# First-stage tiles laid into attention's late tiles, one step of values formed behind attention's first scores, and a changed order of the first loads

## The chip, the cores and the metric

The kernel runs on one core of one Trainium2 chip. The metric is device time in microseconds (us) of one execution, as the median of several. The core has a matrix engine (TensorE, PE in the profile, with PEld for its weight loads), a vector engine (VectorE, DVE), an activation engine (ScalarE, ACT), a general engine (GpSimd, POOL) and SyncE (SP), whose only work here is to issue transfers. SyncE, ScalarE and GpSimd each issue DMAs in the order of their own instruction streams: an instruction that waits holds up everything queued behind it on its engine.

## The reference, cut to what matters

The model has two layers on a feature map x of shape 4 x 384 x 32 x 32. What the change touches is the attention of the first layer, 8 heads of 48 channels, with relative-position tables:

```
x    = x + conv0(_ln_c(x))
xt   = x.reshape(b, c, n).transpose(0, 2, 1)                # _ln_c has been applied
qkv  = (xt @ w_qkv).reshape(b, n, 3, HEADS, hd)             # n = 1024, hd = 48
attn = q*scale @ k^T + gather(q*scale @ table_k^T) + gather(k*scale @ table_q^T)^T
attn = softmax(attn)
out  = attn @ v + (attn summed by relative position) @ table_v
out  = out @ w_proj + b_proj
```

Behind it come a small feed-forward part, a depthwise convolution and a mixture of four experts of which each token takes two. The change leaves their arithmetic alone. The experts' input buffer in DRAM (xs_d) is filled with zeros during attention, and that filling is touched.

## The kernel before, in words

Three phases run one after the other: `qkv_phase`, `attention_phase`, `rest_phase`. All arithmetic is in 32-bit floats.

**`qkv_phase`** goes over the 4096 tokens in 8 steps of 512 (t = 0 to 7 in the code; the texts here say step 1 to step 8). A step loads its tokens `xt` (L155), takes their mean and variance (`token_stats`: PE transposes L87, VectorE L89 and L90, ScalarE's square root L96, VectorE's reciprocal L97), spreads the reciprocal deviation over the partitions (`to_partitions`: VectorE L115 builds a diagonal `s_dg`, PE L117 multiplies it into `all_ps`, ScalarE L168 copies it to `scale`), forms q and k (36 matmuls, L174), scales them on VectorE (L178) into `qk_sb` and stores them to `qk_d` by GpSimd (L179). Then it takes the statistics of the *next* step, and last forms its own v: for each of four blocks of 128 tokens six matmuls (L185) and a ScalarE copy (L188) into `va`, which GpSimd stores to `v_d` (L193, 1 MB a step). The order inside this phase is not written out: the framework's scheduler orders each engine's instructions by readiness in its own model of time, earlier lines first. In the trace it sets two matmuls of v before the last three transposes of the next step's statistics, which wait for a PSUM buffer. The phase's tiles (`wq`, two `va`, three `xt`, `scale`, `s_dg`, four `qk_sb`) live in pools of their own, which end with the phase; so do its PSUM buffers.

**`attention_phase`** goes over 8 heads. Here the order is written out by hand: nearly every instruction goes through `pin`, `mm`, `dma` (SyncE, L226) or `bulk` (ScalarE, L229), which keep it behind the instruction traced before it on its engine. For the first head, `load_tables` and `load_keys` fetch q, k and the tables; `prepare` multiplies q and k with the tables (L221, `tabq_ps` and `tabk_ps`), 32 of each; VectorE transposes one product into the tile `b2` (L316), ScalarE copies the other (L320) into `st`, and SyncE stores it to the DRAM buffer `sd`. Then the head's 32 image rows are worked one by one. For a row:

- `fetch` loads the row's 240 KB from `sd` into `s1` (three buffers) on SyncE, and GpSimd adds it to `b2` (L351, three instructions a row at most) into `bias` (three buffers);
- `queries` loads `qs` for two rows on SyncE (two buffers, so the one for rows 6 and 7 waits for the scores of row 3);
- `scores`: 16 matmuls (L221, `sc_ps`, two PSUM buffers, so the scores of a row wait for `biased` of the row two before);
- `biased`: VectorE adds the bias and takes the minimum (L379) into `arow` (three tiles; rows 0 to 5 and 38 to 43 of each are padding that stays zero);
- `exponentials`: ScalarE (L389); `far_sums`: VectorE (L400); `transposes`: PE L408 and ScalarE L409 into `aT`; `windows`: PE L418 and ScalarE L427 into `a1t`; every fourth row `values`: 64 matmuls with `vb` (L221, `av_ps`).

`load_values` fetches `vb` (four transfers of 256 KB, one for each image of the batch) and `load_value_table` fetches `tvw` (15 transfers, one a row from row 1 on), both on SyncE. `clear` writes zeros to `xs_d`, 64 transfers of 384 KB in all. The tiles `vb`, `aT`, `a1t` and `tvw` of the pool `late` are first written only after the first scores.

The start of a head, before the change:

```
            for s in blk[:3]:
                fetch(s)
            for _ in load_values(h):
                pass
...
            scores(blk[0])
            scores(blk[1])
...
            biased(blk[0])
            exponentials(blk[0])
```

and in the loop over the rows y `queries(blk, y + 4)` (at even y) stands ahead of `fetch(blk[y + 3])`.

Of the kernel before, what the change touches and what calls it, by code (L numbers as in the profile page):

```python
# [11 lines left out]
F32 = mybir.dt.float32  # L12
# [6 lines left out]
P = 128  # L19
# [12 lines left out]
YB = 4  # L32
# [77 lines left out]
def to_partitions(nc, pools, ident, one, values):  # L110

    small, psum, tag = pools
    nj = values.shape[1]
    dg = small.tile([P, nj, P], F32, tag="s_dg", name="s_dg", bufs=1)
    nc.vector.tensor_tensor(dg, bcast(ident.unsqueeze(1), 1, nj), bcast(values, 2, P), ALU.mult)  # L115
    ps = psum.tile([P, TOK], F32, tag=tag, name="all_ps")
    nc.tensor.matmul(ps, one, dg.rearrange("p j n -> p (j n)"), start=True, stop=True)  # L117
    return ps
# [14 lines left out]
def qkv_phase(tc, cst, x, w_qkv, qk_d, v_d):  # L133
# [5 lines left out]
    one, ident = cst["one"], cst["ident"]  # L139
    with ExitStack() as es:  # L140
        wp = es.enter_context(tc.tile_pool(name="q_w", bufs=1))
        work = es.enter_context(tc.tile_pool(name="q_work", bufs=2))
        ev = es.enter_context(tc.tile_pool(name="q_ev", bufs=4))
        psum = es.enter_context(tc.tile_pool(name="q_ps", bufs=3, space=PSUM))
        psmm = es.enter_context(tc.tile_pool(name="q_mm", bufs=4, space=PSUM))
        vas = [wp.tile([P, HEADS, TOK // P, VW], F32, name=f"va{i}") for i in range(2)]
        for va in vas:
            nc.vector.memset(va, 0.0)
        wq = wp.tile([P, KC, 3 * C], F32, name="wq")
        xts = {}  # L150

        def load(t):
            b, n0 = divmod(t * TOK, N)
            xts[t] = work.tile([P, KC, TOK], F32, tag="xt", name="xt", bufs=3)
            nc.sync.dma_start(xts[t], x[b, :, n0 : n0 + TOK].rearrange("(k p) n -> p k n", p=P))  # L155
# [6 lines left out]
        for t in range(NT // TOK):  # L162
# [3 lines left out]
            ps = to_partitions(nc, (work, psum, "st"), ident, one, rstd)  # L166
            scale = work.tile([P, TOK], F32, tag="scale", name="scale")
# [3 lines left out]
            for m in range(2 * KC):  # L171
                ps = psmm.tile([P, TOK], F32, tag="mm", name="qk_ps")
                for k in range(KC):
                    nc.tensor.matmul(  # L174
                        ps, wq[:, k, m * P : (m + 1) * P], xt[:, k, :], start=(k == 0), stop=(k == KC - 1)
                    )
                sb = ev.tile([P, TOK], F32, tag="qk", name="qk_sb")
                nc.vector.tensor_tensor(sb, ps, scale, ALU.mult)  # L178
                nc.gpsimd.dma_start(qk_d[m * P : (m + 1) * P, t * TOK : (t + 1) * TOK], sb)  # L179
            if t + 1 < NT // TOK:  # L180
                stats = result(token_stats(nc, (work, psum, "st"), ident, xts[t + 1], cst["eps6"]))
            for j in range(TOK // P):
                ps = psmm.tile([P, TOK], F32, tag="mm", name="v_ps")
                for k in range(KC):
                    nc.tensor.matmul(  # L185
                        ps[:, :C], xt[:, k, j * P : (j + 1) * P], wq[:, k, 2 * C :], start=(k == 0), stop=(k == KC - 1)
                    )
                nc.scalar.activation(  # L188
                    vas[t % 2][:, :, j, :HD], ps[:, :C].rearrange("p (h d) -> p h d", d=HD),
                    AF.Copy, scale=rstd[:, j, :],  # L190
                )
            w = NBLK // 2 * VW
            nc.gpsimd.dma_start(  # L193
                v_d.rearrange("h p n -> p h n")[:, :, t * w : (t + 1) * w],
                vas[t % 2].rearrange("p h c d -> p h (c d)"),
            )


def attention_phase(tc, cst, held, tabs, tv, qk_d, v_d, ao_d, xs_d, heads):
# [31 lines left out]
    with ExitStack() as es:  # L231
        dram = es.enter_context(tc.tile_pool(name="a_dram", bufs=2, space=DRAM))
        late = es.enter_context(tc.tile_pool(name="a_late", bufs=1))
# [9 lines left out]
        vb = late.tile([P, B, NBLK, VW], F32, name="vb")  # L243
        aT = late.tile([P, NBLK, YB, P], F32, name="aT")
        a1t = late.tile([P, 4, IMG, YT, B], F32, name="a1t")
        tvw = late.tile([P, 4, IMG, HD], F32, name="tvw")
# [11 lines left out]
        zero = fixed.tile([P, 1, C], F32, name="zero")  # L258
        nc.gpsimd.memset(zero, 0.0)
# [262 lines left out]
        def clear():  # L522

            rows = 2 * P
            for n0 in range(0, NEXP * CAP, rows):
                dma(
                    xs_d[n0 : n0 + rows].rearrange("(n p) c -> p n c", p=P), bcast(zero, 1, rows // P),
                )
                yield
# [14 lines left out]
        for n, h in enumerate(heads):  # L544
# [10 lines left out]
            for _ in load_values(h):  # L555
                pass
            if n:
                for g in (1, 2):
                    add_table(batch[1], g, value_table(g, ps_t))
            scores(blk[0])  # L560
            scores(blk[1])
            if n:
                po = value_table(3, ps_o)
            biased(blk[0])
# [8 lines left out]
            for y in range(IMG):  # L573
                s, r = blk[y], y % YT
                if y % 2 == 0 and y + 4 < IMG:
                    queries(blk, y + 4)
                if y + 3 < IMG:
                    fetch(blk[y + 3])
                if batch and y == 3:
# [930 lines left out]
def metaformer_kernel(ctx: ExitStack, tc: tile.TileContext, ins, out):  # L1510
# [19 lines left out]
    with tc.tile_pool(name="held", bufs=1) as pool:  # L1530
# [4 lines left out]
        qkv_phase(tc, cst, ins["x"], ins["w_qkv"], qk_d, v_d)  # L1535
        attention_phase(tc, cst, held, ins["tabs"], ins["tv"], qk_d, v_d, ao_d, xs_d, list(range(HEADS)))
# [72 lines left out]
```

## Time and profile before

| what | us |
|---|---|
| median of 7 runs | 3055.09 (3053.51 to 3068.28) |
| the profiled execution, its own time | 3048.92 |
| its span (first to last instruction) | 3047.2 |
| PE busy in the span | 2917.1 (96%) |
| VectorE, ScalarE, GpSimd busy | 1960.0, 1370.2, 1151.0 |
| last matmul of `qkv_phase` ends | 216.4 |
| table products of the first head | 217.0 to 250.2 |
| first scores of the first head | 250.2 to 252.7 |
| first transposes of the first head start | 261.3 |

How to read it: the profile is of one execution, and its time differs from the median of the runs, so a sum is made inside the profiled execution and then carried to the median. Engine shares are averages over all stages. The timeline gives, by engine, start, duration, operation, `output<-inputs`, the number of instructions merged into the line, and in square brackets how long the engine stood idle before it and what ended that. The chain of waits follows the work that ended last. A "q" behind an engine's name is its queue (instruction stream), as in SPq for an issue of a transfer. Times in the texts are counted from the start of the span.

### The profile page before, as it was taken

The page shows a single profiled execution, that of the slowest core. Times are in us where ns is not written, and L with a number is a line of the kernel's source. Part 1 is how long each engine was busy: PE and PEld are TensorE (multiplying, and loading weights), DVE is VectorE, ACT ScalarE, POOL GpSimd, SP SyncE. Part 2 cuts the span into 40 slices and gives each one's busy share as a digit, 9 for nine tenths or more (in the row PEclk, how much of TensorE's full clock was granted, in tenths as well). Part 3 has the DMA queues.
Part 4 walks back from the last instruction along what each step waited for, and adds up shares of the span by engine and source line. Part 5 has one row for each costly group of instructions (what it writes and reads, how often), then busy time and mean ns, then how long its engine had stood idle before and what let it go on. Part 6 is the DMA issues. An engine that isn't in the chain of part 4 may idle for free.

```text
span 3047.2 us, 63460 instructions
## 1 busy us (share of the span) xinstructions
PE 2917.1 (96%) x25391; PEld 2018.5 (66%) x25391; DVE 1960.0 (64%) x3577; ACT 1370.2 (45%) x2833; POOL 1151.0 (38%) x1123
## 2 busy tenths in 40 slices
PE   9998999999999999999999789999999999999996
PEld 4555777777776777777533347776577777777775
DVE  3237787877787877787578879999899640001101
ACT  1116666676767666666312332433342342233332
POOL 2115556564647473747300212251124231124412
PEclk9998999999999999999999889999999999999998
DMA  4346666666676676665400405724243165357742
GB/s 156 140 144 206 156 216 165 216 162 219 159 220 165 206 176 204 168 207 153 179 21 35 148 13 192 282 102 153 102 162 127 33 226 225 136 221 255 266 180 73
DMA packets 274568, 500.56 MB, mean 164 GB/s; under 512 B 135632, under 2 KB 204112, under 8 KB 266592
## 3 DMA queue, kind: packets, MB, share of 16 engines
q1 hardware_dynamic: 185376, 269.93, 28.8%
q0 software_dynamic: 37792, 202.68, 18.0%
q10 hardware_dynamic: 51104, 23.89, 3.8%
q8 instruction: 200, 3.28, 0.5%
q14 instruction: 96, 0.79, 0.1%
HBM read 543.58 MB, written 152.37 MB: 228 GB/s over the span
## 4 chain that ended last, share of the span: by engine, by line
PE 71%; DVE 13%; issue 7%; DMA 3%; POOL 2%; ACT 2%; SPq 0%; another core or an unknown queue 0%; DVEq 0%; POOLq 0%; ACTq 0%
PE e_ps L1316 12%; PE y_ps L1294 12%; DVE xb L1104 8%; PE t_ps L408 7%; PE av_ps L221 7%; PE sc_ps L221 7%; PE tabq_ps L221 6%; PE qk_ps L174 4%; PE a_ps L418 3%; PE v_ps L185 2%; PE tv_ps L221 2%; PE proj_ps L992 1%; PE tap_ps L1152 1%; PE f_ps L1027 1%; DMA s<-sd 1%
## 5 line engine op out<-in xcount | busy, mean ns | idle before, releaser
L1316 PEld LDWEIGHTS e_ps<-xT,w 128*128 128x128 f32 x4824 | 656.2, 193 | 216.1 <-issue 14.0
L351 POOL TENSOR_TENSOR bias<-b,s 128x416 f32<-128x416 f32 (+24 forms) x656 | 660.0, 1043 | 185.1 <-DMA s<-sd 172.4
L1316 PE MATMUL e_ps<-xT,w 128*128 128x128 f32 x4824 | 670.3, 277 | 12.7 <-ACT xT L1279 4.4
L1294 PE MATMUL y_ps<-w,eh 128*128 128x384 f32 x1608 | 650.4, 490 | 13.6 <-ACT eh L1319 12.4
L1104 DVE SCALAR_TENSOR_TENSOR xb<-img,pack,xb 128x1024 f32<-128x1024 f32 (+1 forms) x539 | 634.3, 1239 | 0.0
L1319 ACT ACTIVATE eh<-e_ps,w 128x128 f32<-128x128 f32 x804 | 293.1, 367 | 717.9 <-PE e_ps L1316 658.2
L1284 POOL DMA_INDIRECT w<-in_w,row x134 | 171.6, 1281 | 739.6 <-PE y_ps L1294 277.0
L400 DVE TENSOR_REDUCE extra<-arow 128x32 f32<-128x32 f32 (+24 forms) x768 | 381.2, 555 | 8.7 <-ACT arow L389 4.9
L379 DVE CUSTOM_DVE_ANT_0 arow<-sc_ps,bias 128x1024 f32<-128x1024 f32 x256 | 312.5, 1221 | 99.3 <-POOL bias L351 50.6
L389 ACT ACTIVATE arow<-arow,nm 128x1024 f32<-128x1024 f32 x256 | 302.3, 1181 | 75.1 <-DVE nm L379 67.4
L408 PEld LDWEIGHTS t_ps<-ident,arow 128*128 128x128 f32 x2048 | 219.7, 141 | 173.3 <-ACT aT L409 100.6
L409 ACT COPY aT<-t_ps 128x512 f32<-128x512 f32 x512 | 278.5, 603 | 92.5 <-PE t_ps L408 92.1
L408 PE MATMUL t_ps<-ident,arow 128*128 128x128 f32 x2048 | 281.5, 281 | 15.8 <-ACT arow L389 15.8
L1297 DVE TENSOR_TENSOR yo<-y_ps,w 128x384 f32<-128x384 f32 x67 | 36.9, 551 | 392.4 <-PE y_ps L1294 387.6
L221 PE MATMUL sc_ps<-kk,qs 48*32 48x512 f32 x4096 | 276.7, 603 | 7.2 <-DVE nm L379 6.0
L1294 PEld LDWEIGHTS y_ps<-w,eh 128*128 128x128 f32 x1608 | 248.0, 193 | 27.1 <-ACT eh L1319 15.4
L221 PEld LDWEIGHTS av_ps<-aT,vb 128*64 128x64 f32 x4096 | 222.3, 137 | 51.3 <-ACT aT L409 41.2
L316 DVE STREAM_TRANSPOSE b<-tabk_ps 128x480 f32<-128x480 f32 x256 | 218.7, 984 | 36.9 <-PE tabk_ps L221 36.9
L221 PE MATMUL av_ps<-aT,vb 128*64 128x128 f32 x4096 | 237.7, 274 | 0.0
L221 PE MATMUL tabq_ps<-tab,kq 48*128 48x480 f32 x512 | 221.1, 581 | 5.1 <-ACT st L320 2.9
L221 PE MATMUL tabk_ps<-tab,kq 48*128 48x480 f32 x512 | 224.2, 585 | 0.0
L221 PEld LDWEIGHTS tabq_ps<-tab,kq 48*128 48x128 f32 x512 | 148.6, 296 | 46.7 <-ACT aT L409 5.5
(210 smaller groups left out, 3129.3 us busy)
## 6 DMA issues: line engine op xcount, KB each, us to landing
sd<-st SPq DMA_DIRECT2D x128, 480.0 KB
s<-sd SPq DMA_DIRECT2D x256, 240.0 KB
xs_d<-zero SPq DMA_DIRECT2D x64, 384.0 KB
tvw<-in_tv SPq DMA_DIRECT2D x120, 192.0 KB
y_d<-yo SPq DMA_DIRECT2D x67, 192.0 KB
qk_d<-qk_sb POOLq DMA_DIRECT2D x48, 256.0 KB
qs<-qk_d SPq DMA_DIRECT2D x256, 48.0 KB
kq<-qk_d ACTq DMA_DIRECT2D x56, 192.0 KB
```

The lines of the kernel that those rows point to most:

```text
L221: ins = nc.tensor.matmul(*args, **kw)
L316: turn = nc.vector.transpose(b2.rearrange("p e y x -> p x (e y)")[:, i + j], ps[:, j, : SPAN * IMG])
L351: nc.gpsimd.tensor_tensor(bias[:, y0:y1, :], bass.AP(b2.tensor, b2.offset + (e * IMG + y0) * IMG, [list(b2.ap[0]), [(step * IMG + 1) * IMG ...
L379: nc.vector.tensor_tensor_reduce(s["flat"], ps.rearrange("p h n -> p (h n)"), s["bias"].rearrange("p y x -> p (y x)"), -SCALE, BIG, ALU.ad ...
L389: nc.scalar.activation(s["flat"], s["flat"], AF.Exp, bias=s["nm"], scale=-1.0, accum_out=dn[:, y % YT : y % YT + 1])
L400: pin(nc.vector.tensor_reduce(ex[:, i, :], a[:, p0:p1, :].rearrange("p y x -> p x y"), AX.X, ALU.add))
L408: pin(nc.tensor.transpose(pt[:, j, :], s["flat"][:, k0 : k0 + P], ident))
L409: pin(nc.scalar.copy(aT[:, 4 * g : 4 * g + 4, s["y"] % YB, :], pt))
L1104: ins_ = nc.vector.scalar_tensor_tensor(acc[:, k, y0:y1], img[:, k, dy + y0 : dy + y1, dx : dx + IMG], w7[:, k, dy, dx : dx + 1], acc[:, k ...
L1294: nc.tensor.matmul(py, hs, w[:, o : o + C], start=(ff == 0), stop=(ff == NF - 1))
L1316: nc.tensor.matmul(ph, w[:, o : o + P], xT[k][:, c, :], start=(c == 0), stop=(c == KC - 1))
L1319: nc.scalar.activation(hs, ph, AF.Gelu, bias=w[:, o : o + 1])
```

## The change

Five things are done.

1. The tiles of `qkv_phase` are no longer tiles of their own. `late` is allocated before the phase, and `wq` and the three `xt` become slices of `a1t`; the two `va`, two `scale` and `s_dg` slices of `tvw`; the four `qk_sb` slices of `vb`.
2. The values of step 7 (t = 6) are not formed in `qkv_phase`. It returns a function that does so, which `attention_phase` calls in the first head after `scores(blk[1])`, ahead of `biased(blk[0])`. Its matmuls are pinned and write PSUM buffers of `ps_t`; its store to `v_d` is issued by ScalarE and pinned, where the other seven steps' is issued by GpSimd. Step 8's values stay where they were.
3. In the first head `load_values` moves from before the first scores to row 1, behind `fetch(blk[4])`.
4. In the first head, up to row 6, `fetch(blk[y + 3])` is issued ahead of `queries(blk, y + 4)`.
5. The tile `zero` is gone. `clear` reads 192 zeros of the padding of `arow[0]`, so that a transfer has 512 pieces of 768 bytes instead of 256 of 1536, and each partition writes two neighbouring rows of `xs_d`.

```diff
@@ qkv_phase
-        vas = [wp.tile([P, HEADS, TOK // P, VW], F32, name=f"va{i}") for i in range(2)]
-        wq = wp.tile([P, KC, 3 * C], F32, name="wq")
+        wq, *xs = views(late["a1t"], [[KC, 3 * C]] + 3 * [[KC, TOK]])
+        *vas, scale0, scale1, dg = views(late["tvw"], 2 * [[HEADS, TOK // P, VW]] + 2 * [[TOK]] + [[TOK // P, P]])
+        evs = views(late["vb"], 4 * [[TOK]])
...
+        def values(t, xt, rstd, pool, keep=lambda ins_: ins_, store=nc.gpsimd.dma_start):
+            for j in range(TOK // P):
+                ps = pool[0].tile([P, TOK], F32, tag=pool[1], name="v_ps")
+                for k in range(KC):
+                    keep(
+                        nc.tensor.matmul(
+                            ps[:, :C], xt[:, k, j * P : (j + 1) * P], wq[:, k, 2 * C :],
+                            start=(k == 0), stop=(k == KC - 1),
+                        )
+                    )
+                nc.scalar.activation(
+                    vas[t % 2][:, :, j, :HD], ps[:, :C].rearrange("p (h d) -> p h d", d=HD),
+                    AF.Copy, scale=rstd[:, j, :],
+                )
+            w = NBLK // 2 * VW
+            store(
+                v_d.rearrange("h p n -> p h n")[:, :, t * w : (t + 1) * w],
+                vas[t % 2].rearrange("p h c d -> p h (c d)"),
+            )
...
-            xts[t] = work.tile([P, KC, TOK], F32, tag="xt", name="xt", bufs=3)
+            xts[t] = xs[t % 3]
...
-            scale = work.tile([P, TOK], F32, tag="scale", name="scale")
+            scale = (scale0, scale1)[t % 2]
...
-                sb = ev.tile([P, TOK], F32, tag="qk", name="qk_sb")
+                sb = evs[(2 * KC * t + m) % 4]
...
+            if t + 2 == NT // TOK:
+                held = t, xt, rstd
+            else:
+                values(t, xt, rstd, (psmm, "mm"))
+
+    return lambda pool, keep, store: values(*held, pool, keep, store)
@@ attention_phase
-        zero = fixed.tile([P, 1, C], F32, name="zero")
-        nc.gpsimd.memset(zero, 0.0)
...
+                zero = arow[0][:, :PADR].rearrange("p y x -> p (y x)").unsqueeze(1)
                 dma(
-                    xs_d[n0 : n0 + rows].rearrange("(n p) c -> p n c", p=P), bcast(zero, 1, rows // P),
+                    xs_d[n0 : n0 + rows].rearrange("(p n) (t c) -> p (n t) c", p=P, t=2),
+                    bcast(zero, 1, 2 * rows // P),
                 )
...
             for s in blk[:3]:
                 fetch(s)
-            for _ in load_values(h):
-                pass
             if n:
+                for _ in load_values(h):
+                    pass
...
             if n:
                 po = value_table(3, ps_o)
+            else:
+                more_values((ps_t, "t"), pin, lambda *ends: pin(nc.scalar.dma_start(*ends)))
             biased(blk[0])
...
-                if y % 2 == 0 and y + 4 < IMG:
+                begun = n or y > 6
+                if begun and y % 2 == 0 and y + 4 < IMG:
                     queries(blk, y + 4)
                 if y + 3 < IMG:
                     fetch(blk[y + 3])
+                if not begun and y % 2 == 0:
+                    queries(blk, y + 4)
+                if not n and y == 1:
+                    for _ in load_values(h):
+                        pass
```

The small tiles of the statistics keep their pool, which now stays open through attention. The order in which rows 1 to 31 call `load_value_table`'s transfers (after the fetch of the row) is unchanged, so at row 1 the first of them stands behind `load_values`.

## The prediction

> **What bounds the kernel now.** The table of busy times gives PE 96% of the span, so I looked for the places where PE stands still, first in the timeline of PE from the last step of the first phase to the first rows of head 1.
>
> ```profile
> 208.44 7.90 PE L185 MATMUL v_ps<-wq,xt 128*128 128x384 f32 x24
> ...
> 251.56 1.09 PE L221 MATMUL sc_ps<-kk,qs 48*32 48x512 f32 x16 [0.30 <-DVE b L316]
> 261.33 1.97 PE L408 MATMUL t_ps<-ident,arow 128*128 128x128 f32 x8 [8.68 <-ACT arow L389]
> 263.23 3.01 PE L221 MATMUL sc_ps<-kk,qs 48*32 48x512 f32 x32
> ```
>
> One step's values cost PE 24 matmuls; the chain of waits puts them at 7.75 us (208.61 to 216.36). After the first scores PE idles 8.68 us, and its next 8 transposes take 1.97 us where row 1's take 1.09. The chain over that gap:
>
> ```profile
> 250.68 2.52 DMA sd<-st
> ...
> 253.72 2.54 DMA s<-sd
> ...
> 256.88 1.87 POOL bias L351
> ...
> 259.93 0.09 DVE nm L379
> ...
> 261.10 0.19 ACT arow L389
> ```
>
> The gap is latency: the last table store lands, row 0 is fetched, GpSimd adds, VectorE adds, ScalarE takes the exponential. PE has nothing to do with it, and the change gives it 7.75 us of matmuls there.
>
> **Part 1, what leaves the first phase.** The timelines of PE and VectorE at step 7:
>
> ```profile
> 183.08 1.15 PE L87 MATMUL row_ps<-ident,xt 128*128 128x128 f32 x9
> 184.06 0.81 PE L185 MATMUL v_ps<-wq,xt 128*128 128x384 f32 x2
> 184.71 0.49 PE L87 MATMUL row_ps<-ident,xt 128*128 128x128 f32 x3
> 185.04 7.26 PE L185 MATMUL v_ps<-wq,xt 128*128 128x384 f32 x22
> 192.13 1.02 PE L117 MATMUL all_ps<-s_dg,one 128*128 128x512 f32 x2
> ```
>
> ```profile
> 186.97 0.69 DVE L115 TENSOR_TENSOR s_dg<-ident,s_rstd 128x512 f32<-128x512 f32 x1
> ```
>
> Without these 24 matmuls PE would come to `all_ps` at 184.5, but its operand ends at 187.66: VectorE is busy throughout (183.28 to 186.3), then square root, reciprocal, diagonal. That is a bubble of 3.1 us, unless step 8's q and k come first; they need only `xt` and a PSUM buffer, of which there are four. The rows show such an overtaking: two of v stand ahead of three older transposes. So I take a bubble of 0 and keep 0 to 3.1. Four buffers hold 4 x 2.57 = 10.3 us of it, and the first scaling can come at about 189.3 (187.7 + 0.86 + 0.58), long before the fifth is wanted. Step 8 and its values then end 7.75 us earlier, at 208.6. Its k must be back from DRAM by then: the last `kq` load was issued at 209.06, after a store that GpSimd issued at 204.48. That store comes 7.8 us earlier, so the load goes at about 201 and lands at 203, 6 us in hand.
>
> Product stage: the same instructions, the same 1 MB store of step 8 beside them, 7.75 us earlier. 0.
>
> **Part 2, what the gap takes in.** From here times are those of the old profile; the new ones are 7.75 earlier. v starts at 252.6 and ends at 260.35; ScalarE's fourth copy (0.58) ends at 260.95. The store on ScalarE waits for it; its issue I put at 0.65, the dearer of ScalarE's two `kk` issues (0.65 and 0.55); bounds 0.3 (SP's shortest) to 0.9 (GpSimd's for this tile). Behind it on ScalarE stands the exponential of row 0, and all rows behind that. It started at 260.04; now 261.65. Transposes of row 0: 263.0 instead of 261.33, 1.6 later. But PE was slow there. The windows view of granted clock, cut at 3.4 us:
>
> ```profile
> 224.50:227.90 3.40, 0.45 (x4) 0.09 (x2) 1.55 (x2) 0.70 (x2) 0.00 (x0) 1.00 0.98 397
> ...
> 251.80:255.20 3.40, 0.86 (x16) 0.00 (x0) 0.00 (x0) 0.16 (x1) 0.00 (x0) 1.00 0.52 175
> ```
>
> (first number after the stretch: its length, then PE busy; PEclk is the third from the end). Each is followed by stretches at 0.50, 255.2 to 265.4 here. The new gap of PE, 260.35 to 263.0, is 2.65 us, against 2.95 and 8.68 that halved the clock and 0.67 that did not. At full clock transposes and scores of row 2 take 2 x 1.02, ending 265.05; VectorE's `biased` of row 2 started at 265.41. So late exponential and full clock cancel: 0. At half clock they end 2 us later: 0 to +2.
>
> The Trainium skill, "TensorE: Matmul & The Clock Gate", section "What's actually happening", says that the clock is halved after an idle window of about 3.4 us that runs freely. Both drops agree in spacing, but each followed a window with 0.45 or 0.86 us of PE work, so the rows are the stricter. By the rule this term is 0; by the rows up to 2 us.
>
> **Part 3, what waits for that store.** It is the change's new wait. In row 1 SP issues the fourth `vb` load (image 3 holds steps 7 and 8) and the first `tvw` load (its slice held `va`); both wait until the store has landed. Behind them on SP stand the fetch of row 5 and the queries of rows 6 and 7; for these wait GpSimd, VectorE and PE. Old rows, from the timelines of SP, GpSimd, VectorE and PE:
>
> ```profile
> 267.65 0.54 SPq L226 DMA_DIRECT2D s<-sd  x1
> ```
>
> ```profile
> 270.65 5.01 POOL L351 TENSOR_TENSOR bias<-b,s 128x384 f32<-128x384 f32 x4 [0.66 <-DMA s<-sd]
> ```
>
> ```profile
> 273.66 1.22 DVE L379 CUSTOM_DVE_ANT_0 arow<-sc_ps,bias 128x1024 f32<-128x1024 f32 x1
> ```
>
> ```profile
> 274.94 1.09 PE L221 MATMUL sc_ps<-kk,qs 48*32 48x512 f32 x16 [0.18 <-DVE nm L379]
> ```
>
> The fetch of row 5 is issued at 267.65; 3.0 us later GpSimd starts on it, takes 2.5, and VectorE takes it with no wait to speak of; the scores of row 7 (the PE line) wait for VectorE. So a fetch later than 267.65 + 0.5 delays PE by the whole rest. When does the store land? The same 1 MB went out from GpSimd at 193.22; the DMA line of that window (192 to 202, 40 slices) shows
>
> ```profile
> DMA  0000000001099999999999819770000007999899
> ```
>
> 1.5 us to the first packet, then some 4.1 us, with one 256 KB store of q and k in it: 310 GB/s. The table stores show 410 GB/s. The new store, issued at 261.0, starts at 262.5 beside row 4's fetch (240 KB) and three `vb` loads (768 KB): 2.0 MB take 4.9 to 6.5 us, so it lands at 267.4 to 269.0; I take 268.2. The two waiting loads take 0.42 each to issue, the fetch goes at 269.1, GpSimd starts at 272.1, VectorE at 274.6 instead of 273.66: **1.0 us lost**, 0.2 to 1.7 by the two rates, and up to 3.2 if the 448 KB now ahead of the fetch delay it fully (448 KB / 310 GB/s = 1.5). The fourth `vb` load lands near 271; the first use is at 275.96.
>
> The Trainium skill, "DMA: Bandwidth & Descriptors", section "Issuing engines are not separate DMA queues", speaks against the store by ScalarE: transfers of all issuers share the same 16 DMA engines, and a second issuer saves only issue time. By that rule the 2.0 MB are one load, as summed. Were the store's path its own, it would land at 266.6 and this term would be 0.
>
> **Part 4, costed at nothing.** Row 3's fetch no longer has 1 MB of `vb` ahead of it (GpSimd waited 1.33 us for it, at 263.65); but its sum ended at 267.5 and VectorE takes it at 268.21, so nothing is gained. The queries of rows 4 and 5 go 1.9 us later (257.61 to about 259.5); the scores that need them come at 267.64: 6 us of cover; past that, each us costs one. Those of rows 6 and 7 go from 266.37 to 269.7 and land at 272.3; the scores of row 6 came at 272.21, just on time. The clear: 64 transfers of the same bytes in twice the pieces. The trace's single packets take 18 ns at 256 bytes, 72 to 78 at 1536 and 105 to 120 at 1920, nearly by size; so 512 of 768 bytes cost about what 256 of 1536 do (1.2 us over 16 engines), doubled at the worst: 64 x 1.2 = 77 us of DMA time, spread over heads 1 to 8 behind fetches that run three rows ahead. I take 0, with an end of 64 x 0.1 = 6 us. The slices themselves are free: nothing of attention wrote `a1t`, `tvw` or `vb` before 255.
>
> **The sum.** -7.75 + 0 (bubble) + 0 (clock) + 1.0 (row 5) = -6.75 us: the profiled execution would go from 3048.92 to 3042.2 (span 3047.2 to 3040.5). The median of the runs stands 6.17 above the profiled execution; I carry the difference over: 3055.09 - 6.75 = 3048.3. A difference under 0.2% (6.1 us) can hardly be told from none here, and the forecast lies just past it.
>
> **Rivals.**
> - *The store takes the gap's place* (chance 0.22). Row 5 comes 3.2 late, and the half clock costs 2: -7.75 + 5.2 = -2.5, 3052.5. For it: SP works in order, and 1.5 us of PE idling may add a slow window. Against: GpSimd's own idle before row 5, 0.66.
> - *The bubble stays* (0.10): the scheduler keeps `all_ps` ahead of q and k. -7.75 + 3.1 + 1.0 = -3.7, 3051.4; if the clock drops too, 3.4 us at half rate add 1.7: 3053.1. Against: the overtaking above.
> - *Slower: waits set by whole tiles* (0.08). `wq` and the three `xt` now lie in one tile; if an access waits for every earlier one of the tile, each step's q and k wait for the next step's load. The chain shows 4.64 us for the first (0.75 to 5.39); seven are 32 us, 25.7 net: 3081. It decides from the second such wait on (2 x 4.64 > 7.75). Against it stands SP's row
>
> ```profile
> 149.21 50.29 SPq L226 DMA_DIRECT2D kq<-qk_d  x2
> ```
>
> where the first loads of `qk_d` go while stores of later steps into the same tensor are still to come, and the four `vb` loads, 0.4 us apart into one tile.
>
> **Chances and range.** Forecast 0.60 (3045.5 to 3051: the sum with its bounds in part 3, or up to 3 us better where the half clock of the products, eight pairs of matmuls at 0.80 instead of 0.40 us, falls away), rivals 0.22, 0.10, 0.08. Faster by over 0.2% (below 3049.0): three quarters of the forecast, 0.45, and a little of the rest: 0.47. Slower: the third rival, 0.08. Within: 0.45. The range runs from 3044 (7.75 + 3.2 gained) to 3057 (first two rivals, and a third of the clear's 6 us); outside lie the slower rival and some luck, under 0.2.
>
> **What would show it.** Step 8's q and k directly behind its statistics, PE's first phase ending at 208.6; 24 `v_ps` behind the first scores; PE's gap there under 3 us and PEclk 1.0 after it; the fetch of row 5 behind a wait for the store, GpSimd's wait before row 5 near 2 us. I am wrong if PE waits before `all_ps` in step 8, if any earlier step grows beyond its 25.36 us, or if the scores of rows 6 and 7 wait over 3 us.

## The result, and the profile after the change

| | before | after |
|---|---|---|
| median of the runs, us | 3053.8 (72 runs, 3046.74 to 3068.28) | 3051.78 (30 runs, 3044.27 to 3057.44) |
| ratio, with its 95% interval | | 0.9991 [0.9985, 0.9998] |
| the profiled execution's own time, span | 3048.92, 3047.2 | 3056.03, 3054.3 |

By the ratio the change gains 2.7 us (0.6 to 4.6); the two medians differ by 2.0. The forecast gain was 6.8: the time lies in the stated range, but well above the forecast, and within 0.2% of before. The two profiled executions stand the other way round than the medians. Their totals can't be compared: from the ninth row of head 1 to the end, with the same work, the span takes 2763.6 before and 2775.3 after, and 2765.3 in a second profile of the changed kernel. So the readings below stop at that ninth row, and count from S, the start of the first scores (250.18 before, 241.39 after).

**The first phase gained what was forecast.** The timeline of PE after the change, at the end of step 7, at the first table product, and behind the first scores:

```profile
183.50 1.15 PE L87 MATMUL row_ps<-ident,a1t 128*128 128x128 f32 x9
184.49 1.02 PE L211 MATMUL qk_ps<-a1t 128*128 128x512 f32 x2
185.35 0.49 PE L87 MATMUL row_ps<-ident,a1t 128*128 128x128 f32 x3
185.67 2.74 PE L211 MATMUL qk_ps<-a1t 128*128 128x512 f32 x6
188.25 1.08 PE L118 MATMUL all_ps<-tvw,one 128*128 128x512 f32 x2
...
209.76 0.77 PE L249 MATMUL tabq_ps<-tab,kq 48*128 48x480 f32 x1 [0.67 <-ACT tvw L179]
...
242.80 1.09 PE L249 MATMUL sc_ps<-kk,qs 48*32 48x512 f32 x16 [0.32 <-DVE b L338]
243.82 8.01 PE L174 MATMUL v_ps<-a1t 128*128 128x384 f32 x24
255.51 1.42 PE L430 MATMUL t_ps<-ident,arow 128*128 128x128 f32 x8 [3.69 <-ACT arow L411]
256.86 3.24 PE L249 MATMUL sc_ps<-kk,qs 48*32 48x512 f32 x32
```

Step 8's q and k (`qk_ps`) overtake the last transposes and fill the time until `all_ps`; there is no bubble. The first product starts at 209.76 instead of 217.02 (7.26 earlier; in the second profile 209.25, 7.77 earlier). The difference between the two lies ahead of the phase's first `all_ps`, which comes at 14.59 before, 15.02 after and 14.50 in the second profile: counted from there, both gain 7.7. Over all the profiles below, the first product starts at 208.95 to 210.21 in the eleven with part 2 and at 216.83 to 217.89 in the three without it. The gap takes in all 24 matmuls. But PE's gap behind them is 3.69 us (in both profiles), where under 3 was forecast.

**The first rows gave half of it back**: from S to the ninth `biased` of VectorE it is 37.65 us instead of 33.46 (37.58 in the second profile). Two chains set this. ScalarE's timeline, before and after:

```profile
250.67 1.28 ACT L389 ACT_TABLE_LOAD   x1
260.04 1.15 ACT L389 ACTIVATE arow<-arow,nm 128x1024 f32<-128x1024 f32 x1 [8.08 <-DVE nm L379]
```

```profile
251.87 0.58 ACT L179 ACTIVATE tvw<-v_ps,s_rstd 128x384 f32<-128x384 f32 x1 [1.35 <-PE v_ps L174]
252.48 0.41 ACTq L589 DMA_DIRECT2D v_d<-tvw  x1
252.92 1.28 ACT L411 ACT_TABLE_LOAD   x1 [0.48 <-ACT tvw L179]
254.22 1.15 ACT L411 ACTIVATE arow<-arow,nm 128x1024 f32<-128x1024 f32 x1
```

*Chain 1, the exponential of row 0.* The load of the exponential's table stands directly ahead of the first exponential in ScalarE's stream. Before, ScalarE reached it in idle time, and 8.08 us of idling followed it. Now four copies of v and a store stand ahead of it, and its 1.28 us fall between the copies and the exponential. That starts at S + 12.83 instead of S + 9.86. PE's gap is long enough that the clock halves after it (third number from the end; the first two are length and PE busy):

```profile
252.73:256.13 3.40, 0.62 (x6) 0.62 (x7) 1.97 (x4) 2.52 (x3) 3.40 (x4) 1.00 0.95 313
256.13:259.53 3.40, 3.40 (x37) 1.07 (x35) 1.52 (x3) 2.31 (x4) 3.28 (x4) 0.50 0.98 278
259.53:262.93 3.40, 3.40 (x48) 1.89 (x32) 3.40 (x6) 2.20 (x5) 1.59 (x2) 1.00 1.08 270
```

It stays at half for 3.4 us (6.8 in the second profile) instead of 10.2 before. The third `biased` comes at S + 17.65 instead of S + 15.23: 2.4 us lost.

*Chain 2, row 5.* SP's, GpSimd's and VectorE's timelines after the change:

```profile
253.58 0.33 SPq L254 DMA_DIRECT2D s<-sd  x1
254.01 4.35 SPq L254 DMA_DIRECT2D vb<-v_d  x4
258.46 0.38 SPq L254 DMA_DIRECT2D tvw<-in_tv  x1
258.94 0.37 SPq L254 DMA_DIRECT2D s<-sd  x1
```

```profile
266.49 2.51 POOL L373 TENSOR_TENSOR bias<-b,s 128x384 f32<-128x384 f32 x2 [5.37 <-DMA s<-sd]
```

```profile
269.04 1.23 DVE L401 CUSTOM_DVE_ANT_0 arow<-sc_ps,bias 128x1024 f32<-128x1024 f32 x1 [1.52 <-POOL bias L373]
```

The fetch of row 5 (the second `s<-sd`) is issued at S + 17.55, as before (S + 17.48). SP's wait for the store, inside the 4.35 us of the `vb` issues, costs little here: when the fetch is issued at 258.94, the `vb` loads ahead of it are still moving. But GpSimd can start on the row only 7.55 us later, at S + 25.10 (S + 20.47 before), and VectorE waits for it. By the trace's packets, ScalarE's store runs from 253.79 to 257.49; the fetch of row 4, issued at 253.58, moves from 257.00 on, and the `vb` loads, issued from 254.01 on, from 257.61 to 262.78. Row 5's fetch lies behind them in SP's queue. In the second profile row 5 starts at S + 23.85, so this mark moves by 1.25 us between two executions of one kernel; what a single profile below adds or takes away at row 5 has to be read against that.

### The profile page after: what moved, and what is told of

It is laid out like the page before. It is cut to its first block, busy times and chain, and to the rows that moved or that the text cites. A ratio compares the mean times of both kernels' runs of the same rounds, so it can differ in the third digit from the quotient of the medians.

```text
span 3054.3 us, 63467 instructions
## 1 busy us (share of the span) xinstructions
PE 2924.0 (96%) x25391; PEld 2020.3 (66%) x25391; DVE 1958.6 (64%) x3577; ACT 1372.6 (45%) x2833; POOL 1162.2 (38%) x1121
## 4 chain that ended last, share of the span: by engine, by line
PE 75%; DVE 14%; issue 4%; DMA 3%; ACT 2%; POOL 2%; SPq 0%; POOLq 0%; DVEq 0%; ACTq 0%
PE e_ps L1348 13%; PE y_ps L1326 13%; DVE xb L1136 8%; PE t_ps L430 8%; PE av_ps L249 7%; PE sc_ps L249 7%; PE tabq_ps L249 6%; PE qk_ps L211 4%; PE a_ps L440 3%; PE v_ps L174 2%; PE tv_ps L249 2%; PE proj_ps L1024 1%; PE f_ps L1059 1%; PE tap_ps L1184 1%; PE o_ps L1063 1%
```

## The experiments

The kernel before was timed again beside every group of runs and its median moved between the groups (3039.77 beside the first four experiments, 3056.05 beside the next four, 3052.73 beside the last four). So only ratios compare. One per mille is 3.1 us. The table has the marks of the profiles, counted from S; "exp" is the start of row 0's exponential, "row 5" the start of GpSimd's sum for it.

| kernel | exp | biased row 2 | row 5 | biased row 5 | biased row 8 | ratio |
|---|---|---|---|---|---|---|
| before | 9.86 | 15.23 | 20.47 | 23.48 | 33.46 | 1 |
| after | 12.83 | 17.65 | 25.10 | 27.65 | 37.65 | 0.9991 |
| after_again | 12.85 | 18.22 | 23.85 | 27.59 | 37.58 | 0.9991 |
| e1_clear_alone | 9.70 | 15.07 | 20.44 | 23.29 | 33.29 | 0.9996 |
| e2_vb_behind_row5 | 12.84 | 17.26 | 19.76 | 26.19 | 37.71 | 1.0004 |
| e3_store_gpsimd | 12.35 | 16.40 | 31.29 | 33.81 | 44.95 | 1.0012 |
| e4_store_early | 12.37 | 17.37 | 23.16 | 25.74 | 35.74 | 0.9989 |
| e5_code_shift | 12.86 | 17.38 | 25.49 | 28.05 | 38.04 | 1.0000 |
| e6_table_early | 11.56 | 15.48 | 24.79 | 27.32 | 39.58 | 0.9995 |
| e7_vb_split | 12.84 | 17.33 | 23.12 | 27.61 | 37.62 | 0.9981 |
| e8_all_three | 11.56 | 15.19 | 23.18 | 25.70 | 39.57 | 0.9993 |
| e9_values_in_place | 9.86 | 15.23 | 22.31 | 24.85 | 34.86 | 1.0010 |
| e10_row5_first | 12.84 | 17.45 | 19.42 | 26.11 | 36.11 | 0.9990 |
| e11_row5_first_all | 11.59 | 15.22 | 18.66 | 23.43 | 33.43 | 0.9989 |

### The clear alone (e1)

The kernel before, with part 5 of the change and nothing else:

```diff
-                    xs_d[n0 : n0 + rows].rearrange("(n p) c -> p n c", p=P), bcast(zero, 1, rows // P),
+                zero = arow[0][:, :PADR].rearrange("p y x -> p (y x)").unsqueeze(1)
+                    xs_d[n0 : n0 + rows].rearrange("(p n) (t c) -> p (n t) c", p=P, t=2),
+                    bcast(zero, 1, 2 * rows // P),
```

> The kernel before with part 5 alone: the clear reads the padding of arow[0] in 512 pieces of 768 bytes. Theory A (the local gain of head 1 is 4.6 to 5.0 us and part of it is given back later by the clear's smaller pieces): the whole kernel is 2 to 3 us slower than before. Rival B (the clear costs nothing; what lies between the local gain and the median is scatter of other stages): within 1 us of before, ratio 1.000 with an interval that holds 1.

Measured: 0.9996 [0.9982, 1.0009], 33.29 to row 8. The clear costs nothing that can be seen. The interval alone would allow up to 2.7 us, but the clear's transfers are spread over the heads, and from row 8 of head 1 to the last row of head 8 this kernel takes 1178.5 us, the one before 1178.4. So the clear did not eat the gain.

### Values left in place (e9)

The changed kernel without its part 2:

```diff
-            if t + 2 == NT // TOK:
+            held = t, xt, rstd
+            if t < 0:
                 held = t, xt, rstd
             else:
                 values(t, xt, rstd, (psmm, "mm"))
...
             else:
-                more_values((ps_t, "t"), pin, lambda *ends: pin(nc.scalar.dma_start(*ends)))
+                pass
```

> The changed kernel with step 7's values left in the first phase and stored there by GpSimd; the slices, the order of the first loads (vb in row 1, fetches ahead of queries) and the clear from the padding stay. Theory A (the gain is the 24 matmuls that leave the first phase, and the slices, load order and clear are worth nothing by themselves): the first table product starts at about 217 as before, no bubble and no longer step in the first phase; the first scores to the ninth biased row take 33 to 34 us as before (33.46), since no store stands in ScalarE's queue and no exponential is late; time within 0.2% of before, ratio 0.9985 to 1.0015. Theory B (the slices cost something, for example a load of tokens that waits for the whole tile, or the vb loads in row 1 hold row 5 back even without the store): the first phase grows beyond 217.5 or the stretch beyond 35 us, and the ratio is above 1.001.

Measured: 1.0010 [0.9999, 1.0022]. The first product starts at 216.83, so the slices cost the first phase nothing. But row 8 comes at 34.86, where 33 to 34 was expected. SP's and GpSimd's timelines tell why:

```profile
261.39 1.82 SPq L255 DMA_DIRECT2D vb<-v_d  x4
263.27 0.42 SPq L255 DMA_DIRECT2D tvw<-in_tv  x1
263.79 0.36 SPq L255 DMA_DIRECT2D s<-sd  x1
```

```profile
272.24 12.84 POOL L374 TENSOR_TENSOR bias<-b,s 128x384 f32<-128x384 f32 x13 [3.88 <-DMA s<-sd]
```

Nothing waits for a store here and row 5's fetch is issued 3.6 us earlier than before (S + 13.87), yet GpSimd starts on it 8.45 us after its issue. With 1 MB of `vb` loads directly ahead of that fetch (part 3), the stretch is 1.4 us longer than before, with no late store and no late exponential.

### The vb loads behind row 5 (e2)

```diff
-                if not n and y == 1:
+                if not n and y == 2:
                     for _ in load_values(h):
```

> The changed kernel with the four vb loads moved from row 1 to row 2, behind the fetch of row 5 and the queries of rows 6 and 7. Theory A (the loss in head 1 comes from row 5's fetch, which stands in SP's queue behind 1 MB of vb that starts only when the ScalarE store has ended): from the first product matmul to the scores of row 7 59.0 us instead of 60.56 (before: 57.92), GpSimd's wait before row 5 gone, the kernel some 1.5 to 2.5 us faster than the changed one. Rival B (SP's wait for the landing of the store is what delays row 5): the first tvw load still waits for it ahead of row 5's fetch, so the time stays at 60.56. If vb then comes late for the first values of row 3, PE waits there instead, by up to 2 us.

Measured: 1.0004 [0.9993, 1.0014]. SP still waits for the store (at the tvw load), and its fetch of row 5 goes at 259.54. Now GpSimd starts on it 3.2 us later, and next has to wait for row 6, which has the four `vb` loads ahead of it instead:

```profile
262.73 2.52 POOL L373 TENSOR_TENSOR bias<-b,s 128x384 f32<-128x384 f32 x2 [0.27 <-DMA s<-sd]
272.91 9.12 POOL L373 TENSOR_TENSOR bias<-b,s 128x416 f32<-128x416 f32 x10 [7.66 <-DMA s<-sd]
```

So the fetch takes 3.2 us with no `vb` load ahead of it (4.9 in e10, where the store's packets are still moving when it is issued) and 7.55 with all four. The wait moved by one row, and row 8 stayed where it was (37.71).

### The store by GpSimd, and the store taken out of the gap (e3, e4)

e3 issues step 7's store on GpSimd:

```diff
-                more_values((ps_t, "t"), pin, lambda *ends: pin(nc.scalar.dma_start(*ends)))
+                more_values((ps_t, "t"), pin, nc.gpsimd.dma_start)
```

> The changed kernel with step 7's values stored by GpSimd, not by ScalarE, behind its sum of row 3. Theory A (packets of ScalarE's queue hold back those of SP's queue, as in the changed kernel's trace, where row 4's fetch is issued at 253.58 and moves from 257.00 on): with the software queue of GpSimd the two run side by side, row 4's fetch moves within 2 us of its issue; but the store goes out some 4 us later, behind row 3's sum, so the fourth vb load and all behind it on SP come later, and the scores of row 7 come 2 to 4 us later than in the changed kernel. Rival B (all queues share and the order of issue alone counts): row 4's fetch is held back as before.

Measured: 1.0012 [0.9998, 1.0025]. The store is issued at 261.75, behind GpSimd's sum for row 4; SP's fourth `vb` load waits for it, and row 5 starts at S + 31.29. Here SP's wait does decide; the stretch grows to 44.95.

e4 has no store in the gap. The same 1 MB goes out at step 7, from what the tile then holds, so this kernel leaves step 7's values out of `v_d`:

```diff
                 held = t, xt, rstd
+                w = NBLK // 2 * VW
+                nc.gpsimd.dma_start(
+                    v_d.rearrange("h p n -> p h n")[:, :, t * w : (t + 1) * w],
+                    vas[t % 2].rearrange("p h c d -> p h (c d)"),
+                )
...
-                more_values((ps_t, "t"), pin, lambda *ends: pin(nc.scalar.dma_start(*ends)))
+                more_values((ps_t, "t"), pin, lambda *ends: None)
```

> The changed kernel with the late store left out: the same 1 MB is stored by GpSimd at step 7 in the first phase, from what the tile then holds (step 5's values), so step 7's values in the output are not the reference's. Matmuls and ScalarE copies of step 7 stay behind the first scores. Theory A (the store holds back rows 4 and 5 and vb): rows 4 and 5 are fetched as fast as in the kernel before, the scores of row 7 come 57.9 to 58.9 us after the first product matmul (changed: 60.56), the kernel 2 to 2.7 us faster than the changed one. Rival B (the loss comes from PE's gap and its half clock, not from the store): 60 us or more.

Measured: 0.9989 [0.9978, 1.0000]. Row 5 starts at S + 23.16 instead of 25.10 (23.85 in the second profile), and row 8 comes at 35.74: by these profiles the store is worth 1.9 us of the 4.2. The other 2.3 us are there without it.

### Three terms taken away one by one (e5, e6, e7)

e5 shifts the instruction stream of PE by 12 tiny matmuls at the start (the reason stands in the last section):

```diff
+        pad_ps = psum.tile([P, TOK], F32, tag="st", name="pad_ps")
+        for _ in range(12):
+            nc.tensor.matmul(pad_ps[:32, :32], one[:, :32], one[:, :32], start=True, stop=True)
```

> The changed kernel with 12 small matmuls (32x32, results unused) at the very start, where PE waits for the first load: 48 more PE instructions ahead of the products, as many as the change takes away there. Theory A (the last table store lands late because a 16 KB transfer of PE's instructions, which the moved matmuls have shifted, takes one of the 16 DMA engines just then): that transfer comes some 4 us before the last table store again, and from the first scores to the first sum on VectorE (row 0) it is 8.4 to 8.7 us (before 8.60, changed 9.75; 9.6 to 9.8 in the three variants so far); the scores of row 7 and all behind come about 1.1 us sooner. Rival B (the table stores pile up because the change puts other transfers beside them): 9.6 to 9.8 as in the changed kernel.

Measured: 1.0000 [0.9987, 1.0013]. VectorE's first `biased` comes at S + 8.66 as before, instead of S + 9.75. But the exponential still starts at S + 12.86: the copies of v cover it. No gain.

e6 lets ScalarE load the exponential's table ahead of the copies:

```diff
+                early = small.tile([P, 1], F32, tag="nm", name="early")
+                nc.vector.memset(early, 0.0)
+                pin(nc.scalar.activation(early, early, AF.Exp))
                 more_values((ps_t, "t"), pin, lambda *ends: pin(nc.scalar.dma_start(*ends)))
```

> The changed kernel with one exponential of a 128x1 tile ahead of step 7's ScalarE copies, so that the 1.28 us load of the exponential's table happens while ScalarE waits for PE. Theory A (the exponential of row 0 is late by the copies, the store's issue and the table load, which stood in idle time before): row 0's transposes come 1.2 us sooner; from VectorE's sum of row 0 to that of row 2 it is 6.6 us (before 6.63, changed 7.90), less if PE's gap then stays below what halves its clock. Rival B (row 2 is late only by PE's half clock): 7.5 us or more, since PE's gap of 2.4 us is still long.

Measured: 0.9995 [0.9981, 1.0009]. ScalarE's timeline has the exponential directly behind the store's issue, and GpSimd's shows what is late instead:

```profile
252.65 0.41 ACTq L592 DMA_DIRECT2D v_d<-tvw  x1
253.11 1.15 ACT L411 ACTIVATE arow<-arow,nm 128x1024 f32<-128x1024 f32 x1 [0.49 <-ACT tvw L179]
```

```profile
266.34 2.49 POOL L373 TENSOR_TENSOR bias<-b,s 128x384 f32<-128x384 f32 x2 [4.98 <-DMA s<-sd]
```

Chain 1 is whole again (biased row 2 at S + 15.48, 2.2 us better than after), but row 5 comes about as late as it did (S + 24.79), and what was won is waited away there. Row 8 is even later (39.58), since PE next waits 2.07 us for the queries of row 6 and the clock halves once more.

e7 puts three of the four `vb` loads back ahead of the first scores; only image 3, which needs the late store, stays in row 1:

```diff
-        def load_values(h):
-            for b in range(B):
+        def load_values(h, bs=range(B)):
+            for b in bs:
...
             for s in blk[:3]:
                 fetch(s)
+            for _ in load_values(h, range(B) if n else range(B - 1)):
+                pass
...
                 if not n and y == 1:
-                    for _ in load_values(h):
+                    for _ in load_values(h, range(B - 1, B)):
```

> The changed kernel with three of the four vb loads (images 0 to 2, which need no value of step 7) back ahead of the first scores, right behind the fetches of rows 0 to 2; the fourth stays at row 1. Theory A (row 5 is late by the store and by the 768 KB of vb that run after it): from VectorE's sum of row 2 to the scores of row 7 it is 9.5 to 10.2 us (before 9.53, changed 11.28), the kernel 1.1 to 1.7 us faster than the changed one. Rival B (SP's wait for the store's landing decides): 11 us or more, since the fourth vb load and the first tvw load still wait for it ahead of row 5.

Measured: 0.9981 [0.9970, 0.9992], the lowest ratio of all. Its profile does not explain that: row 5 starts at S + 23.12, 2 us earlier than after, but the clock stays at half for 6.8 us from 257.79 on, chain 1 is late, and row 8 comes at 37.62 as after.

### All three, and row 5 ahead (e8, e10, e11)

e8 joins e5, e6 and e7.

> The changed kernel with all three edits: small matmuls at the start, the table load ahead of the copies, three vb loads back ahead of the scores. Theory A (these are three separate losses of 1.1, 1.3 and 1.5 us): from the first scores to VectorE's sum of row 8 it is 33.5 to 34 us (before 33.46 without the 7.75 us of step 7's values, changed 37.65), so that the whole 7.7 us of the first phase is kept: the kernel 6.5 to 7.5 us faster than before, ratio 0.998. Rival B (each edit only uncovers the next wait): 36 us or more, ratio 0.999.

Measured: 0.9993 [0.9977, 1.0010]. Biased row 2 is back at S + 15.19, but then PE waits for the queries of rows 6 and 7, which lie behind the fourth `vb` load, a tvw load and row 5 in SP's stream; the clock halves after that wait:

```profile
267.24 2.21 PE L252 MATMUL sc_ps<-kk,qs 48*32 48x512 f32 x16 [3.61 <-DMA qs<-qk_d]
```

e10 is e7 with the fourth `vb` load and the first tvw load behind row 5's fetch and those queries; e11 adds the edits of e5 and e6:

```diff
-                if not n and y == 1:
+                if not n and y == 2:
                     for _ in load_values(h, range(B - 1, B)):
                         pass
...
-                if y:
+                if y > 1 or n and y:
+                    next(pieces, None)
+                if not n and y == 7:
                     next(pieces, None)
```

> As the split of the vb loads (three of four before the first scores, the fourth later), and now the fourth vb load and the first tvw piece stand in row 2, behind row 5's fetch and the queries of rows 6 and 7; the tvw piece that is missing is made up in row 7. So nothing that SP issues ahead of row 5's fetch waits for the store. Theory A (SP's wait for the store decides): row 5's fetch goes as soon as its buffer is free, about 259.9, and lands 3 us later; GpSimd's wait before row 5 falls from 3.2 to under 1 us, the scores of row 7 come 9.5 to 10 us after the biased row 2 (11.57 with the split alone, 9.53 before), and the ratio is 0.9965 to 0.998. Theory B (the store's packets and the other loads fill the DMA engines, whatever waits are set): the fetch lands no earlier than about 265, or the queries of rows 6 and 7 or the fourth vb load become the wait, the stretch stays above 11 us or the next one grows by as much, and the ratio is 0.998 to 0.9995.

Measured: 0.9990 [0.9978, 1.0002]. SP's timeline has the fetches of rows 4 and 5 in one group with no wait for the store between them, then the queries:

```profile
254.75 2.78 SPq L254 DMA_DIRECT2D s<-sd  x2
261.49 1.19 SPq L254 DMA_DIRECT2D qs<-qk_d  x2
262.87 0.45 SPq L254 DMA_DIRECT2D vb<-v_d  x1
```

Row 5 starts at S + 19.42, earlier than before the change. Chain 2 is gone, and the stretch falls by 1.5 us against e7, to 36.11: what is left of the loss, 2.65 us, is chain 1.

> As the run before, with the 12 small matmuls at the start that shift the instruction fetch, and the exponential's table loaded ahead of the copies of v. Theory A (three separate terms of about 1.1, 1.3 and 1.8 us): biased row 0 comes 8.6 to 8.7 us after the first scores, biased row 2 6 to 6.6 us after that, the scores of row 7 9.5 to 10.2 us after that, and from the first scores to the ninth biased row it is 34 to 35 us (33.46 before, 37.65 after the change); ratio 0.996 to 0.998, with the 12 matmuls costing at most 0.5 us of it. Theory B (each edit only uncovers the next wait): the stretch stays above 36 us, since with earlier rows the queries of rows 6 and 7 or the vb loads come late, and the ratio is no better than the run before.

Measured: 0.9989 [0.9978, 1.0001]. With both chains mended, PE's gap is 2.45 us and the clock stays whole:

```profile
254.66 1.09 PE L433 MATMUL t_ps<-ident,arow 128*128 128x128 f32 x8 [2.45 <-ACT arow L414]
255.69 1.95 PE L252 MATMUL sc_ps<-kk,qs 48*32 48x512 f32 x32
```

Row 8 comes at S + 33.43, as before the change (33.46): the two chains account for all of the 4.2 us. This is one profile, and part of it is luck: a gap of nearly this length halved the clock in e6 (last section). In the profiles row 8 comes at 275.20, against 283.64 before and 279.04 after. The total doesn't show it: -3.4 us (-6.7 to +0.3), where the first product gains 6.8 us and row 8 8.4 (1.6 of these in the product stage, by its clock).

### The change once more (after_again)

The changed kernel with no edit, beside e9, e10 and e11.

> The changed kernel itself once more, timed beside the three others on the same chip. If the whole of the first phase's 7.7 us less what the first rows give back (4.2 us) is what lasts, the ratio is 0.9985 to 0.9995; if the first rows' loss depends on the execution, the profile's stretch from the first scores to the ninth biased row differs by more than 1 us from 37.65.

Measured: 0.9991 [0.9981, 1.0001]. The stretch is 37.58 against 37.65, but made up otherwise: row 5 starts 1.25 us earlier than in the first profile and VectorE does not wait for it, but the clock stays at half twice as long (6.8 us). There chain 1 sets the stretch, in the first profile chain 2 does.

## Why the prediction came out as it did

- **Part 1, right.** -7.75 with a bubble of 0; measured 7.26 and 7.77 between single profiles (7.7 in both from the first `all_ps` on), and no bubble.
- **Part 2, wrong: "late exponential and full clock cancel: 0".** The step counted copies (to the last copy's end it was within 0.3 us) and the store's issue (0.65 taken, 0.41 measured), but not the table load of 1.28 us that the exponential brings with it; before, it stood in idle time. So PE's gap was 3.69 us instead of 2.65 and the clock halved again. Measured +2.4 (3.0 in the second profile), beyond the +2 that was the end. Without the load the step was nearly right: row 2 is 0.25 us late in e6, with 3.4 us of half clock, and on time in e8 and e11 with full clock (S + 15.19 and 15.22, before 15.23). But the step took full clock for granted behind a gap of 2.65 us, and e6 has half clock behind one of 2.40. The Trainium skill, "ScalarE: Activation LUTs", section "What ACT_TABLE_LOAD costs", gives 1283 ns for the load and a drain of about 1380 ns besides. The trace agrees with the first; of the drain it shows nothing: taking the load away moved the exponential from S + 12.83 to S + 11.56, 1.27 us.
- **Part 3, the place right, the mechanism wrong.** The step had "the fetch goes at 269.1, GpSimd starts at 272.1": a late issue (1.45 us) and 3.0 us of transfer. The issue was on time (0.07 us late) and the transfer took 7.55 us. The row is late only where `vb` loads stand ahead of its fetch: with the store and no unfinished `vb` load it is on time (e2, e10, e11), with `vb` and no late store 1.8 or 2.7 us late (e9, e4), with both 4.6 (3.4 in the second profile). So the loads are shown to be needed for the delay; how much the store adds is less sure. The prediction asked what row 3 gains when the loads move away from it, but left their delay of row 5 at an end of the range (1.5 us for 448 KB). It summed the bytes as one load on shared engines. The Trainium skill, "DMA: Bandwidth & Descriptors", section "Issuing engines are not separate DMA queues", has transfers of different issuers interleave. In this trace they hardly do: SP's fetch of row 4, issued 0.21 us before the store's first packet, moved none until 257.00, 3.4 us later, when the store was nearly through.
- **Part 4, right for the clear** (e1): its packets of 768 bytes took 40 ns each on the mean, where those of 1536 bytes had taken 71. No run has the order of fetches and queries alone; in e9 row 5's fetch goes 3.6 us earlier, and the `vb` loads ahead of it take that back.
- **The sum.** Parts 2 and 3 are not added: a late exponential makes room for a late row 5. Together they took 4.2 us (1.0 forecast), so -7.75 + 4.2 = -3.6, inside the measured -4.6 to -0.6. The rival "the store takes the gap's place" came nearest (-2.5): it named both the half clock and a late row 5, but not the table load behind the one, and of the `vb` loads behind the other it counted only the last (in the 448 KB). The median of 3051.78 lies outside the forecast's own 3045.5 to 3051; it lies in the stated range because that took in this rival's loss, and not because the steps of the forecast held. Neither the bubble nor whole-tile waits were seen.

**Left open.** Whether the change itself loses anything in heads 2 to 8: from row 8 of head 1 to the last row of head 8 the twelve profiles of changed kernels take 1178.0 to 1184.7 us (mean 1180.9), the two of before and e1 1178.4 and 1178.5. In six of the twelve the clock halves once or twice on the way, in before and e1 never: counted from row 8 to row 8, a head with such a drop takes 157.9 to 159.9 us, one without 154.8 to 157.6. Two profiles are too few to say that the change brings these drops. That scatter is as large as what is left to explain, also of the low ratio of e7 and of what e11 should have gained more. No run beats the changed kernel beyond doubt: the interval of e7 overlaps that of after.

## What to carry to other kernels

When work is moved into a gap, list everything that the instruction behind it brings along, its table load among them: what was free in idle time goes onto the path. Count a transfer from its issue to its first packet and not only by bytes over a rate, and look at what is queued ahead of it on both issuing engines. Where two chains end within a us or two of each other, mending one shows little of its worth (e6 and e7 left row 8 no earlier, e10 gained 1.5 us); only the edits together (e11) brought the whole stretch back.

## What was unexpected of the hardware

- **A code fetch delays a store.** VectorE's first `biased` was 1.15 us late after S because the last table store landed late; the waits of SP for it, before and after:

```profile
SPq L226 <- DMA sd<-st: 2.1, 1, 2.1
```

```profile
SPq L254 <- DMA sd<-st: 3.2, 1, 3.2
```

  By the packets, a 16 KB instruction fetch took one of the 16 DMA engines from 242.36 to 243.44, just behind the store's issue at 241.86; before, it came four us ahead of that issue. Taking 24 matmuls and their 24 weight loads out of the first phase had shifted it. e5, which puts as many PE instructions in at the start, moved it away and the wait with it (2.1 us again); that it is PE's own fetch is inferred from this. In the eight profiles with the fetch just behind that store's issue the first `biased` comes at S + 9.5 to 9.9, in the six others at S + 8.4 to 8.8. The copies of v covered the delay, so it cost nothing here.
- **A gap of 2.4 us halves the clock or not, by where it falls.** After gaps of 2.43 and 2.45 us (e8, e11) it stayed whole; after 2.40 (e6) it was halved for 3.4 us, from 256.04 on. After 3.69 it was halved in both profiles of the changed kernel, for 3.4 and for 6.8 us. In each profile all changes of the clock lie a whole number of 3.41 us apart. Cut by that measure, the profiles between 210 and 280 us show a border: at full clock, every stretch with at most 1.88 us of PE work was followed by half clock, and every one with 1.97 or more was not (of the two at 1.89 and 1.90 one each). In e6 the gap falls into one stretch, with 1.63 us of work; in e11 it is split over two, with 1.98 and 2.39. Later in the span the border is less sharp.
- **The table products take one of two times.** Half clock falls into them for 3.4 or for 6.8 us, and their stage takes 31.0 to 32.1 or 33.1 to 33.9 us. Both occur with part 2 of the change and without it.
